# Zeroing PSUM tiles by matrix products and dealing a projection out in pairs, in a relational graph convolution on one Trainium2 core

## The chip, the cores and the metric

The kernel runs on one core of one Trainium2 chip (trn2). The metric is device time in microseconds (us) of one execution. Eight runs of the kernel before the change have a median of 3025.92 us (3016.6 to 3031.64). For this kernel a difference of about 0.2% (6 us) is what a measurement can tell from no change.

The engines are called PE (TensorE, the matrix products, with PEld for its weight loads), DVE (VectorE), ACT (ScalarE), POOL (GpSimd) and SP (SyncE, which here only issues DMAs). Matrix products land in PSUM.

## The reference

Two layers of a relational graph convolution with a residual, then a mixture of experts. N = 6250 nodes of D = 256 features, E = 100000 edges sorted by target, R = 8 relations; everything is f32.

```
seg  = dst * R + etype
sums = segment_sum(x[src], seg, N * R)            # one sum per (target node, relation)
cnt  = segment_sum(ones, seg, N * R)
mean = (sums / max(cnt, 1)).reshape(N, R, D)
y    = x @ Wroot + b + einsum('nrd,rde->ne', mean, W)
```

The first layer takes the layer norm of the input and ends in a relu, the second takes the first one's result. `h = x + y2` is then normalised again; a gate of 8 experts picks the best two of each row, and the weighted outputs of their two-layer networks (256 to 1024 to 256, with gelu) are added to `h`.

## The kernel before, in words

**Preparation** (until about 83 us). Nodes are normalised, each f32 row is split into three bf16 parts whose sum is the row, and these rows of 3 x 256 go to a table in DRAM (`xs`). The edges are turned into columns of indices.

**The two layers** (`layer(k)`, k = 0 from about 83 to 1156 us and k = 1 from there to about 2215 us). The edges lie in 782 tiles of 128 each, and the tiles in 194 groups of 1 to 6. The sums of a group span a window of at most 64 neighbouring nodes. For a group three things happen.

- `tiles_in` (L668 to L688) runs one group ahead of the sums. It takes one of two PSUM tiles `pg` and has ACT copy zeros into it (L672). For every edge tile POOL issues an indirect DMA (L680) that gathers the 128 source rows into one of 13 buffers `ge`, and DVE compares the tile's targets with a ramp (L686), which makes a matrix `oh` with a one where an edge meets its node and relation.
- `sums` (L691 to L700): for each edge tile, PE multiplies `ge` with `oh` in six products (two halves of the features, three bf16 parts; L696). All of them add to `pg`. In layer 0 a seventh product with a block of ones as weights (`ones16`, 128 x 128) makes the counts (L699). A product has 8 columns for each node of its tile's window, 140 on average.
- `add` (L702 to L715): DVE adds the window of `pg` to one of two rings of sums in SBUF (L710). The rings keep 3 blocks of 128 nodes each.

**A block of nodes** is projected when its sums are whole. The planner `_plan` reckons for every one of the 49 blocks the step (a step is one group) from which no later edge can reach it; this is `whole[b]`. Work on a block is due at fixed distances from that step: `root` at -1 (its own features), `counts` at 0, `invert` at 1, then at 2 `project`, `clear` and `finish`, at 3 `turn`, and at 4 `logits`. `project` (L770 to L795) is 18 f32 products of 128 x 256 for a full block, the root and 8 relations with two halves each, in five PSUM tiles `pr` of two relations (L783); two such tiles exist. DVE scales and adds them up in `h` (L791, L793). `clear` has ACT zero the block's part of the ring (L800). `finish` applies the relu and writes the block's rows for the next layer, or the output.

**The main loop** runs over the steps. In a step it first calls `tiles_in` of the next group, then `project` and `clear`, `turn`, `finish`, then `sums` of the step's group, `invert`, `logits`, `add`, and `root`, `counts`. That is the order in which the program states the work. The framework that builds the kernel gives every engine a stream of its own and orders it by when it reckons instructions to be ready; an engine's stream is then fixed, and an instruction that waits holds up all behind it in its stream. `bounds` in `_plan` says which blocks a group may touch; the kernel checks the edges against it before it takes this path, and dependencies that the bounds rule out are not waited for.

**The experts** follow from about 2215 us to the end, with 1024-wide f32 products (L1214, L1225).

Of the kernel before, what the change touches and what calls it, by code (L numbers as in the profile page):

```python
# [39 lines left out]
BF16 = mybir.dt.bfloat16  # L40
# [8 lines left out]
P = 128  # L49
# [45 lines left out]
Z = 4.8  # L95
WIN = 64
RB = 3
READ = 2
TAKE = 3
EARLY = 30  # L100

# [1 line left out]
def _plan(N, E, R):  # L103

    T = -(-E // P)

    def windows(ts, n):

        mid = n // 2
        lo, hi = [0] * n, [-(1 << 30)] * n
        for t in ts:
            for k in range(n + 1):
                i0, i1 = t * P, max(0, t + k - mid) * P
                mean = N * (i1 * i1 - i0 * i0) / (E * E)
                sd = 2 * N * i0 / (E * E) * math.sqrt(abs(i1 - i0)) + 0.004 * abs(mean)
                if k < n:
                    lo[k] = min(lo[k] if t != ts[0] else 1 << 30, math.floor(mean - Z * sd) - (k < mid))
                if k:  # L120
                    hi[k - 1] = max(hi[k - 1], math.ceil(mean + Z * sd) + (1 if k <= mid else 2))
        shift = -min(lo)
        w = [(a + shift, b + shift) for a, b in zip(lo, hi)]
        return shift, w, max(b for _, b in w)


    NB = -(-N // P)
    mid = max(0, round((N / 4 - P / 2) / P))
    split = round(T * math.sqrt((mid + 0.5) * P / N))
    regions = []  # L130
    t = 0
    while t < T:
        left = (split if t < split else T) - t
        for n in range(min(6, left), 0, -1):
            ng = max(1, min(36, left) // n)
            shift, w, width = windows((t + n // 2, t + n * (ng - 1) + n // 2), n)
            if width <= WIN:
                break
        regions.append((t, n, ng, shift, w, width))
        t += n * ng  # L140
    groups = []
    for r, (t0, n, ng, *_) in enumerate(regions):
        for g in range(ng):
            groups.append((t0 + g * n, n, r))
    NG = len(groups)
    up = [g for g in range(NG) if groups[g][0] < split]
    down = list(range(NG - 1, len(up) - 1, -1))
    size = [sum(groups[g][1] for g in s) for s in (up, down)]
    seq, at, n = [], [0, 0], [0, 0]
    while len(seq) < NG:  # L150

        s = int(n[1] * (size[0] - EARLY) < n[0] * size[1])
        if at[s] == len((up, down)[s]):
            s = 1 - s
        g = (up, down)[s][at[s]]
        seq.append(g)
        at[s] += 1
        n[s] += groups[g][1]
    step = {g: q for q, g in enumerate(seq)}

    whole = []
    for b in range(NB):
        if b == mid:
            whole.append(NG - 1)
            continue
        p = math.sqrt((b + 1 if b < mid else b) * P / N)
        dev = Z * math.sqrt(E * p * (1 - p)) + 1
        t = int(min(E - 1, E * p + dev) // P) if b < mid else int((E * p - dev) // P)
        whole.append(step[next(g for g, (t0, n, _) in enumerate(groups) if t0 + n > t)])


    bounds = []
    for g in range(NG):
        read, taken = ([b for b in range(NB) if whole[b] + n < step[g]] for n in (READ - 1, TAKE))
        if g < len(up):
            bounds.append((sum(b < mid for b in read) or -NB, sum(b < mid for b in taken) + RB))
        else:
            n = sum(b > mid for b in read)
            bounds.append((NB - sum(b > mid for b in taken) - RB, NB - n if n else 2 * NB))
    return T, regions, groups, seq, len(up), mid, whole, bounds  # L180
# [3 lines left out]
def kernel(  # L184
# [20 lines left out]
    nc = tc.nc  # L205
# [430 lines left out]
    with tc.If(go == 1) as cmp:  # L636
        with ExitStack() as arm:
# [4 lines left out]
            hTs = ap.tile([P, NB, KD, P], F32, name="hTs", bufs=1)  # L642
            zeros = ap.tile([P, WIN], F32, name="zeros", bufs=1)
            nc.vector.memset(zeros, 0.0)
            rings = [ap.tile([P, KD + 1, R, RING + WIN], F32, name=f"ring{i}", bufs=1) for i in range(2)]

            step = {g: q for q, g in enumerate(seq)}
# [8 lines left out]
            def layer(k):  # L656
# [11 lines left out]
                def tiles_in(g):  # L668
                    t0, n, r = groups[g]
                    pg = psum.tile([P, nd, R, WIN], F32, name="pg", tag="pg", bufs=2)  # L670
                    wd = regions[r][5]
                    state["zeroed"] = nc.scalar.copy(pg[:, :nd, :, :wd],  # L672
                                                     zeros[:, None, None, :wd].to_broadcast([P, nd, R, wd]))
                    got = []
                    ohs = ap.tile([P, OHW], BF16, name="oh", bufs=3)
                    o0 = 0
# [13 lines left out]

                def sums(g):  # L691
                    pg, got = state[g]
                    for ge, oh, m, a, b in got:
                        for c in range(KD):
                            for s in range(3):
                                nc.tensor.matmul(pg[:, c, :, a:b], ge[:m, s, c, :], oh, start=False, stop=False,  # L696
                                                 skip_group_check=True)
                        if nd > KD:
                            nc.tensor.matmul(pg[:, KD, :, a:b], ones16[:m], oh, start=False, stop=False,  # L699
                                             skip_group_check=True)  # L700

                def add(g):  # L702
                    pg, _ = state.pop(g)
# [59 lines left out]
                def invert(b):  # L763
                    if k == 0:
# [2 lines left out]
                        nc.vector.tensor_scalar(invs[:, b], pc[:, :R], 1.0, None, op0=OP.max)  # L767
                        nc.vector.reciprocal(invs[:, b], invs[:, b])

                def project(b):  # L770

                    n = rows(b)
# [3 lines left out]
                    h = ap.tile([P, D], F32, name="h", bufs=2)  # L776
                    lhs = [(R, [xT[:, c, :n] for c in range(KD)])]
                    lhs += [(r, [ring[:, c, r, s0 : s0 + n] for c in range(KD)]) for r in range(R)]
                    for i in range(0, R + 1, 2):
                        pr = psum.tile([P, 2, D], F32, name="pr", tag="mm", bufs=MM)  # L780
                        for j, (r, chunks) in enumerate(lhs[i : i + 2]):
                            for c in range(KD):
# [5 lines left out]
                        for j, (r, _) in enumerate(lhs[i : i + 2]):  # L788
# [3 lines left out]
                            else:  # L792
                                nc.vector.scalar_tensor_tensor(h[:n], pr[:n, j], invs[:n, b, r : r + 1], h[:n],  # L793
                                                               op0=OP.mult, op1=OP.add)
                    state["h", b] = h  # L795

                def clear(b):
# [47 lines left out]
                tiles_in(seq[0])  # L845
                due = {}
                for b, q in enumerate(whole):
                    for d, f in ((-1, root), (0, counts), (1, invert), (2, project), (2, clear), (2, finish), (3, turn), (4, logits)):
                        due.setdefault(q + d, []).append((f, b))

                todo = []
# [8 lines left out]
                def run(q, *fs):  # L860
                    for f, b in due.get(q, []):
                        if f in fs:
                            f(b)

                cleared[:] = [[(-1, ins) for _, ins in c] for c in cleared]
                for q in range(NG + 5):
                    if k == 1 and q == 2:

                        with tc.issue_after(state["zeroed"].ins):
# [4 lines left out]
                    if q == 0 and k == 0:  # L874
                        for c in range(KD + 1):
                            nc.vector.memset(rings[0][:, c], 0.0)
                            nc.scalar.copy(rings[1][:, c], zeros[:, None, 0:1].to_broadcast([P, R, RING + WIN]))
                    run(q, project, clear)
                    run(q, turn)
                    run(q, finish)  # L880
                    if q < NG:
                        sums(seq[q])
                    run(q, invert, logits)
                    if q < NG:
                        add(seq[q])
# [388 lines left out]
```

## Time and profile before

The profiled execution took 3019.99 us; its span, from the first to the last instruction, is 3018.2 us.

| | value |
|---|---|
| median of 8 runs | 3025.92 us |
| profiled execution, and its span | 3019.99 us, 3018.2 us |
| first gather of layer 0 and end of its last | 83.38 us, 1117.38 us |
| first gather of layer 1 and end of its last | 1155.50 us, 2154.01 us |
| gathers in each layer | 782 |
| ACT copies of zeros to `pg` (L672) | 388, 380.1 us in all, 981 ns each |
| ACT clears of the rings (L800) | 98, 227.8 us in all |
| counts products (L699) | 782, 241 ns each by their records |
| granted PE clock, mean over the span | 0.924 |

The granted clock is the share of full speed that PE was allowed at that moment. A record of a product runs from its start to its modelled end, so that records of a stream overlap: what a product costs a busy PE is read from one start to the next.

### The profile page before, as it was taken

The numbers are of one execution on the slowest core, as the hardware profiler recorded it, in microseconds if no ns is written. First come the engines' busy times: TensorE is split into PE (matmuls) and PEld (weight loads), VectorE is DVE, ScalarE is ACT, GpSimd is POOL, SyncE is SP. The second block draws the span as 40 slices with busy tenths as digits, with TensorE's granted clock in tenths as the row PEclk, the third lists the DMA queues.
The fourth block names the chain that finished last, engine by engine and source line by source line (L and its number), as shares of the span: only waits on it lengthen the run. The fifth ranks groups of instructions, "written<-read, shape, count | busy, mean of one in ns | idle before, by whom it ended". The sixth has DMA issues, their size and how long they took to land. (4 is left out here: it accounts for less than half of the span.)

```text
span 3018.2 us, 52037 instructions
## 1 busy us (share of the span) xinstructions
PE 2556.7 (85%) x18131; PEld 2160.1 (72%) x18131; DVE 1620.5 (54%) x4676; ACT 1019.1 (34%) x1378; POOL 1807.3 (60%) x2109
## 2 busy tenths in 40 slices
PE   5578887888889876888888888898839999999997
PEld 2466776776777765666766767777628888888886
DVE  7566676766666674666766776676711111111111
ACT  6434444443444332332323323232312222222221
POOL 1667777777776765777777777777413333333332
PEclk9689999999999997988989998999969999999999
DMA  7555665655565544666566666666364444444441
GB/s 250 156 147 166 169 173 165 171 163 169 166 175 159 163 138 142 177 176 173 167 173 176 173 177 174 174 183 173 109 201 113 118 109 107 109 120 107 107 122 19
DMA packets 215591, 461.05 MB, mean 153 GB/s; under 512 B 50716, under 2 KB 123222, under 8 KB 215190
## 3 DMA queue, kind: packets, MB, share of 16 engines
q0 software_dynamic: 120384, 334.45, 41.9%
q1 hardware_dynamic: 83724, 112.33, 11.2%
q10 hardware_dynamic: 11210, 10.81, 1.1%
q8 instruction: 149, 2.44, 0.3%
q14 instruction: 124, 1.02, 0.1%
HBM read 412.02 MB, written 46.31 MB: 152 GB/s over the span
## 5 line engine op out<-in xcount | busy, mean ns | idle before, releaser
L680 POOL DMA_INDIRECT ge<-xs,idx x1564 | 1518.2, 971 | 618.4 <-issue 224.3
L696 PE MATMUL pg<-oh,ge 128*128 128x200 bf16 (+24 forms) x9384 | 831.9, 241 | 308.7 <-DMA ge<-xs,idx 218.7
L696 PEld LDWEIGHTS <-ge 128*128 128x128 bf16 x9384 | 673.6, 105 | 431.4 <-DMA ge<-xs,idx 270.2
L783 PE MATMUL pr<-gw,ring 128*128 128x256 f32 (+1 forms) x3136 | 747.2, 393 | 1.3 <-DVE h L793 0.8
L783 PEld LDWEIGHTS pr<-gw,ring 128*128 128x128 f32 (+1 forms) x3136 | 612.1, 198 | 96.2 <-DVE h L793 4.7
L710 DVE TENSOR_TENSOR ring<-pg,ring 128x1176 f32 (+31 forms) x388 | 456.5, 1176 | 281.8 <-PE pg L696 141.5
L672 ACT COPY pg<-zeros 128x1176 f32<-128x1176 f32 (+31 forms) x388 | 380.1, 981 | 534.9 <-DVE ring L710 508.5
L793 DVE SCALAR_TENSOR_TENSOR h<-pr,invs,h 128x256 f32<-128x256 f32 (+1 forms) x784 | 376.5, 480 | 157.7 <-PE pr L783 140.0
L800 ACT COPY ring<-zeros 128x3072 f32<-128x3072 f32 (+1 forms) x98 | 227.8, 2324 | 675.3 <-PE pr L783 616.9
L1215 ACT ACTIVATE hT<-ph,bcol 128x256 f32<-128x256 f32 x424 | 200.8, 474 | 536.2 <-PE ph L1214 536.2
L1214 PE MATMUL ph<-xT,w 128*128 128x256 f32 x1696 | 378.2, 382 | 0.0
L1225 PE MATMUL po<-fw,hT 128*128 x1696 | 374.4, 379 | 0.0
L1225 PEld LDWEIGHTS po<-fw,hT 128*128 128x128 f32 x1696 | 322.2, 190 | 43.8
L1214 PEld LDWEIGHTS ph<-xT,w 128*128 128x128 f32 x1696 | 320.9, 192 | 42.2
L686 DVE TENSOR_SCALAR oh<-iota,rel 128x152 bf16<-128x152 f16 (+25 forms) x1564 | 335.9, 273 | 19.4 <-PE pg L699 14.1
L1186 POOL DMA_INDIRECT xg<-xnd,ti x106 | 105.4, 995 | 351.5 <-DMA ti<-tlist 264.8
L1230 POOL DMA_INDIRECT out_dram<-fo,ti x106 | 168.7, 1591 | 229.0 <-DVE wt L1199 108.3
L1228 DVE TENSOR_TENSOR fo<-po,b2b 128x256 f32<-128x256 f32 x106 | 45.0, 425 | 299.5 <-PE po L1225 299.5
L699 PE MATMUL pg<-oh,ones 128*128 128x128 bf16 (+24 forms) x782 | 188.5, 241 | 0.0
L1209 DVE COPY bcol<-b1c 128x8 f32 x53 | 9.0, 171 | 302.4 <-ACT hT L1215 301.9
L699 PEld LDWEIGHTS <-ones 128*128 128x128 bf16 x782 | 82.7, 106 | 2.7
L783 PE MATMUL pr<-gw,hTs 128*128 128x256 f32 (+1 forms) x196 | 70.8, 485 | 2.3 <-ACT hTs L831 2.1
(190 smaller groups left out, 1349.2 us busy)
## 6 DMA issues: line engine op xcount, KB each, us to landing
w<-in_L_ffn_W_dram SPq DMA_DIRECT2D x53, 1024.0 KB
ge<-xs,idx POOLq DMA_INDIRECT x1564
xt<-in_x_dram SPq DMA_DIRECT2D x96, 128.0 KB
xs<-xb SPq DMA_DIRECT2D x8, 1152.0 KB
xs<-hb SPq DMA_DIRECT2D x48, 192.0 KB
fw<-in_L_ffn_W_dram ACTq DMA_DIRECT2D x8, 1024.0 KB
xt<-in_x_dram SPq DMA_DIRECT2D x8, 768.0 KB
out_dram<-h SPq DMA_DIRECT2D x48, 128.0 KB
```

Source lines behind the costliest of these rows:

```text
L672: state["zeroed"] = nc.scalar.copy(pg[:, :nd, :, :wd], zeros[:, None, None, :wd].to_broadcast([P, nd, R, wd]))
L680: nc.gpsimd.indirect_dma_start(out=ge[:m].rearrange("p s k d -> p (s k d)"), out_offset=None, in_=xs[k][:, :], in_offset=bass.IndirectOffs ...
L686: nc.vector.tensor_scalar(oh, iota16[:m].rearrange("p (r d) -> p r d", r=R)[:, :, a:b], rel[:m, t : t + 1], None, op0=OP.is_equal)
L696: nc.tensor.matmul(pg[:, c, :, a:b], ge[:m, s, c, :], oh, start=False, stop=False, skip_group_check=True)
L699: nc.tensor.matmul(pg[:, KD, :, a:b], ones16[:m], oh, start=False, stop=False, skip_group_check=True)
L710: a = nc.vector.tensor_tensor(slot, pg[:, :nd, :, :wd], slot, OP.add).ins
L783: mm = nc.tensor.matmul(pr[:n, j], chunks[c], w[:, c, r, :], start=(c == 0), stop=(c == KD - 1))
L793: nc.vector.scalar_tensor_tensor(h[:n], pr[:n, j], invs[:n, b, r : r + 1], h[:n], op0=OP.mult, op1=OP.add)
L800: ins = nc.scalar.copy(at, zeros[:, None, None, 0:1].to_broadcast([P, nd, R, P]))
L1214: nc.tensor.matmul(ph[:, :TK], w1[:, k, h * P : (h + 1) * P], xT[:, k, :], start=(k == 0), stop=(k == KD - 1))
L1215: nc.scalar.activation(hT[:, h, :], ph[:, :TK], AF.Gelu, bias=bcol[:, h : h + 1], scale=1.0)
L1225: nc.tensor.matmul(po[:, :D], hT[:, k, f * P : (f + 1) * P], rhs, start=(k == 0), stop=(k == KH - 1))
```

## The change

Four edits belong together.

1. `tiles_in` has ACT zero `pg` only in the first three steps of a layer. From step 3 on, `sums` begins with one product for each slice of `pg` (three in layer 0, two in layer 1): `ones16` as weights and a tile of bf16 zeros as columns, with `start=True`, so that the slice is overwritten with zeros. Its width is 8 times the group's window, up to 512 columns.
2. The counts product takes one column of `ones16` as weights in place of all 128, and writes one row of `pg`.
3. `project` no longer issues its products; it puts five pairs of relations in a list. `sums` takes one pair from the list after each edge tile, and what is left is done when the group's tiles are through.
4. `project` is stated after `turn`, `clear` and `finish`; `clear` and `finish` move to distance 3, `turn` to 4 and `logits` to 5, and the loop has one step more. The planner counts a block as read one step earlier (`READ` goes) and leaves a quarter of a tile as margin in `whole`.

```diff
-READ = 2
-        dev = Z * math.sqrt(E * p * (1 - p)) + 1
+        dev = Z * math.sqrt(E * p * (1 - p)) + P / 4
-        read, taken = ([b for b in range(NB) if whole[b] + n < step[g]] for n in (READ - 1, TAKE))
+        read, taken = ([b for b in range(NB) if whole[b] + n < step[g]] for n in (0, TAKE))
+            zeros16 = ap.tile([P, R * WIN], BF16, name="zeros16", bufs=1)
+            nc.vector.memset(zeros16, 0.0)
...
-                    state["zeroed"] = nc.scalar.copy(pg[:, :nd, :, :wd],
-                                                     zeros[:, None, None, :wd].to_broadcast([P, nd, R, wd]))
+                    if step[g] < 3:
+                        state["zeroed"] = nc.scalar.copy(pg[:, :nd, :, :wd],
+                                                         zeros[:, None, None, :wd].to_broadcast([P, nd, R, wd]))
...
                 def sums(g):
                     pg, got = state[g]
+                    wd = regions[groups[g][2]][5]
+                    for c in range(nd if step[g] >= 3 else 0):
+                        nc.tensor.matmul(pg[:, c, :, :wd], ones16, zeros16[:, : R * wd].rearrange("p (r d) -> p r d", r=R),
+                                         start=True, stop=False, skip_group_check=True)
...
-                            nc.tensor.matmul(pg[:, KD, :, a:b], ones16[:m], oh, start=False, stop=False,
+                            nc.tensor.matmul(pg[0:1, KD, :, a:b], ones16[:m, 0:1], oh, start=False, stop=False,
                                              skip_group_check=True)
+                        go_on()
...
+                pairs = []
+                def go_on():
+                    if pairs:
+                        f, i = pairs.pop(0)
+                        f(i)
...
-                    for i in range(0, R + 1, 2):
+                    def pair(i):
                         pr = psum.tile([P, 2, D], F32, name="pr", tag="mm", bufs=MM)
...
+                    pairs.extend((pair, i) for i in range(0, R + 1, 2))
...
-                    for d, f in ((-1, root), (0, counts), (1, invert), (2, project), (2, clear), (2, finish), (3, turn), (4, logits)):
+                    for d, f in ((-1, root), (0, counts), (1, invert), (2, project), (3, clear), (3, finish), (4, turn), (5, logits)):
...
-                for q in range(NG + 5):
+                for q in range(NG + 6):
...
-                    run(q, project, clear)
-                    run(q, turn)
+                    run(q, turn, clear)
                     run(q, finish)
+                    run(q, project)
                     if q < NG:
                         sums(seq[q])
+                    while pairs:
+                        go_on()
```

With the new margin, `whole` moves for 2 of the 49 blocks, by one step each; the groups and their order stay as they are.

## The prediction

> **What bounds the kernel now.** I read the page first, its busy table, then the group of the gathers, then the busy time of each engine by windows that cut the two layers and the experts apart.
>
> ```profile
> PE 2556.7 (85%) x18131; PEld 2160.1 (72%) x18131; DVE 1620.5 (54%) x4676; ACT 1019.1 (34%) x1378; POOL 1807.3 (60%) x2109
> ...
> L680 POOL DMA_INDIRECT ge<-xs,idx x1564 | 1518.2, 971 | 618.4 <-issue 224.3
> ```
>
> PE looks like the bound and POOL like a bystander, but these are averages over three stages. In the timeline a gather takes 0.95 us and the next starts 0.30 us behind its end, whatever else happens: one per 1.25 us. 782 of them are 977.5 us, and a layer's gathers span 1034.0 us (83.38 to 1117.38) and 998.5 us (1155.50 to 2154.01). So **both layers run at the pace of POOL**. What they lose above it is small: in layer 0, 36 gathers longer than 1 us (24.2 us more than 0.95 each) and 31.2 us in which POOL waited beyond its 0.30 us for PE to give back a gather buffer; in layer 1, 12.4 us and 7.3 us. The largest of these waits is
>
> ```profile
> 948.18 0.94 POOL L680 DMA_INDIRECT ge<-xs,idx  x1 [6.37 <-PE pg L696]
> ```
>
> Only these 38.5 us can be won by a better order on PE, and only as long as PE keeps up. Does it? The windows of layer 0 (columns: length, busy of PE, PEld, DVE, ACT, POOL, then granted clock, DMA share, GB/s):
>
> ```profile
> 83.00:200.00 117.00, 79.11 (x652) 64.64 (x652) 71.23 (x149) 48.77 (x51) 81.19 (x83) 0.76 0.52 148
> ...
> 800.00:1000.00 200.00, 172.54 (x1498) 148.62 (x1495) 137.65 (x330) 85.27 (x96) 147.31 (x154) 0.94 0.60 169
> 1000.00:1117.00 117.00, 100.82 (x792) 86.45 (x793) 80.01 (x181) 44.71 (x46) 87.67 (x85) 0.91 0.56 155
> ...
> 2215.00:3018.00 803.00, 761.36 (x3604) 668.35 (x3604) 138.00 (x422) 202.06 (x425) 274.12 (x212) 0.97 0.44 114
> ```
>
> PE is busy 858 of 1034 us in layer 0 (the six windows from 83 to 1117 added up) and 836 of 998 in layer 1. It has 176 and 162 us to spare. The clock is low where PE idles (0.76 in the first window) and 0.97 where it hardly does (the experts), so more work raises it.
>
> **Part 1: zeros by products.** Out go 191 ACT copies in each layer (388 of 981 ns, less three in each layer that stay). ACT is 34% busy, so its time is worth nothing; what counts is who waits for it. PE does, 64.5 us in 60 waits in layer 0 and 14.6 us in 17 in layer 1:
>
> ```profile
> PE pg L696 <- ACT pg L672: 64.5, 60, 4.5
> ```
>
> Some of this wait is ACT standing in its queue before a clear of the ring that waits for a projection. It goes, but it is PE time that the gathers mostly hide, so the gain is a share of the 38.5 us. In come 191 x 3 = 573 products in layer 0 and 382 in layer 1. Their width is that of the additions (L710): by the planner's windows 392 columns on average. Price of a column, from six products of 160 in a stream:
>
> ```profile
> 949.37 0.58 PE L696 MATMUL pg<-oh,ge 128*128 128x160 bf16 x6
> ...
> 949.79 0.23 PE L699 MATMUL pg<-oh,ones 128*128 128x160 bf16 x1
> ```
>
> Six starts take 0.42 us: 0.07 us for 160 columns, 0.172 us for 392. That is **98 us more on PE in layer 0 and 66 in layer 1**. Upper end: the record of a bf16 product of 512 columns (L521, 402 ns with its modelled end), 230 and 154 us. Lower end: the ACT waits that go, taken off whole, 34 and 51 us. I take 98 and 66, because a busy PE pays starts and not records. What is new is the wait: a zeroing product waits for the addition of the group two before, and everything on PE is queued behind it, sums and pairs alike, and behind them the gather buffers. ACT waited for the same addition before and then took 1 us more, so for PE the wait gets shorter; it costs nothing while PE runs ahead of the gathers and up to some 0.5 us a group where it doesn't.
>
> **Part 2: the counts with one column of weights.** It looks like a saving: 782 products in layer 0 with less to load. The trace has the same form in the expert choice (L383, one column of `ones`), between products with 128 columns of weights:
>
> ```profile
> 2041.15 0.19 PE L380 MATMUL rpp<-roh,upper 128*128 128x64 bf16 x1
> ...
> 2041.18 0.18 PE L381 MATMUL rpp<-roh,ones 128*128 128x32 bf16 x1
> 2041.29 0.09 PEld L383 LDWEIGHTS <-ones 128*1 128x1 bf16 x2
> 2041.29 0.20 PE L383 MATMUL rpp<-roh,ones 128*1 128x32 bf16 x2
> ...
> 2041.43 0.25 PE L696 MATMUL pg<-oh,ge 128*128 128x168 bf16 x1
> ```
>
> L381 starts 0.03 us behind L380, whose 64 columns it has to let pass. L383 has only 32 columns to let pass and starts 0.11 us behind L381: its weight load isn't pulled ahead but begins when the array has run out. The next wide product starts 0.12 us behind the second L383 (2041.31; the two share a row). So going in costs 0.08 us more and coming out 0.09. L411 (8 columns of weights, also among L696) shows the same:
>
> ```profile
> 2116.01 0.34 PE L696 MATMUL pg<-oh,ge 128*128 128x184 bf16 x2
> ...
> 2116.27 0.08 PEld L411 LDWEIGHTS <-rnum 128*8 128x8 bf16 x1 [0.15 <-issue]
> 2116.28 0.22 PE L411 MATMUL rpl<-rcol,rnum 128*8 128x128 bf16 x1
> ...
> 2116.43 0.25 PE L696 MATMUL pg<-oh,ge 128*128 128x176 bf16 x1
> ```
>
> The second L696 starts at 2116.09 and needs 0.08 us; L411 comes at 2116.28, 0.11 late, and what follows it 0.10 late. A count in its new form therefore costs PE 0.17 to 0.21 us more than one with 128 columns, whose load (L699) lies in the shadow of the product before. I take 0.18: **141 us more on PE in layer 0**, none in layer 1, which has no counts. Ends: the weight load alone is 24 ns shorter (81 for 105), 19 us less; 0.21 us is 164 more.
>
> The Trainium skill, page "TensorE: Matmul & The Clock Gate", section "LDWEIGHTS (loading the stationary operand)", lets a weight load's time go with its columns (columns / 1.2 ns): one column would be an estimated 1 ns, and by that the change would save some 0.1 us a tile. The record of 81 ns speaks against it. The same page, section "Weight-path perf modes", says that the fast weight load needs 128 weights, which speaks against this edit; it gives no price for leaving it.
>
> **Part 3: pairs between tiles, and the later steps.** The same 18 products for a block and the same DVE work, in another order. A block's products take 36 records of 0.22 us, 7.9 us of PE in which gathers fill six of 13 buffers; with tiles in between, buffers come back earlier. In the stream of the changed kernel as built that is so for groups of five and six tiles; small groups do two pairs or three after their last tile. In the kernel before, the builder had mixed projections and sums in part already. The later `finish` and `turn` spare PE its waits for the relu (L830 on L808, 15.7 us in layer 0). All of this can win from the same 38.5 us. At the seam of the layers (38.1 us from the last gather to the next first one) and behind layer 1 the steps hang on the last block's chain; I count nothing there, within 3 us. The memset of `zeros16` is one small DVE instruction before the layers, under 0.5 us.
>
> **The sum.** Layer 0: PE has 858 + 98 + 141 = 1097 us of work at a clock of 0.92. With PE idle no more the clock should come near the experts' 0.97, so the old 858 shrink by 858 x (1 - 0.92/0.97) = 44, to 1053 us in all. POOL needs 977.5 + 24.2 = 1002. So **PE becomes the bound of layer 0**. Waits that aren't for gathers stay with it: the counts' transfer before a transpose (11.3 us), the first gathers (some 5), additions that zeroing waits for (say 14): 30. That makes 1083 us from the first gather to the last sum; before, it was 1038 (83.4 to 1121.5). Layer 0: +45. Layer 1: 836 + 66 = 902 us of PE against POOL's 990: still POOL's, with 7.3 us of buffer waits that may go or double: 0. Experts: 0. The profiled execution's 3020.0 would become 3065; the median of the runs lies 5.9 above that execution, which gives 3071. I say **3070**.
>
> **Rivals.**
> - **A, the forecast (0.62):** PE-bound layer 0, +20 to +80: 3045 to 3105.
> - **B, faster (0.15):** the narrow count costs next to nothing among the sums, because loads still overlap there. PE then has 858 + 98 - 44, about 912 us, and POOL keeps the layer; of the 38.5 us of buffer waits, half or more go: -20, 3006 (3000 to 3018). It decides from a round trip of about 0.06 us: 47 us more, under which PE's sum and waits stay below 1002. For it: L383 and L411 are few and sit at switches of work. Against it: both show the gap on both sides, and L411 sits among the very sums.
> - **C, near nothing (0.10):** half the price, 0.09 us a tile: PE at about 985 plus 30 of waits against POOL's 1002, gains and losses about even: 3020 to 3045.
> - **D, much slower (0.13):** in layer 0 PE also stands before zeroing products, because DVE, in order and two thirds busy (137.65 of 200), has comparisons and block sums ahead of the addition. 0.5 us on each of 191 groups is 95 us on top: 3105 to 3165. Layer 1 would add to it if its densest stretch goes past POOL's pace.
> - That pairs aren't dealt out as said is part of A: the builder orders them, and the order wins at most the 38.5 us.
>
> Range: A, C and the nearer part of D, 3018 to 3120; B (0.15) and the far end of D (0.04) are left out. About 0.2% (6 us) is what a measurement can tell from no change. Faster: B, 0.15. Same: the lower part of C, 0.06. Slower: 0.79.
>
> **What would show it.** In the new profile: POOL's waits for PE in layer 0 several times 31 us, the gathers' span there near 1080, PE's idle time in that layer gone and its clock above 0.92; count products that start 0.1 us late and are followed 0.1 us late; layer 1's gathers still within 10 us of 998. Wrong: a layer 0 at 1010 to 1030 us with 0.06 us steps around the counts (B), or PE waiting over 60 us for additions (D).

## The result, and the profile after

The changed kernel takes **3047.31 us** (median of 14 runs, 3039.05 to 3052.17), beside 3026.14 us (40 runs) for the kernel before. The ratio is 1.0069, with an interval of 1.0059 to 1.0079: slower by some 21 us. The forecast was 3070, so the sign and the stage were right; the forecast loss of 44 us was about twice the measured one. The profiled execution took 3046.83 us, its span is 3045.1 us (before: 3019.99 and 3018.2).

By stages, both profiled executions, from the first and last gathers on POOL and the last sum on PE:

| stage | before | after | difference | forecast |
|---|---|---|---|---|
| up to the first gather of layer 0 | 83.4 | 82.5 | -0.9 | 0 |
| layer 0, first gather to last sum | 1038.3 | 1072.9 | +34.6 | +45 |
| last sum to first gather of layer 1 | 33.8 | 29.8 | -4.0 | 0 |
| gathers of layer 1 | 998.5 | 989.8 | -8.7 | 0 |
| from there to the end | 864.2 | 870.1 | +5.9 | 0 |
| span | 3018.2 | 3045.1 | +26.9 | +45 |

The page of the changed kernel: the busy table, the chain that ended last by engine and by line, and the gathers, the counts and the zeroing products among the groups.

```profile
PE 2759.3 (91%) x19068; PEld 2190.5 (72%) x19086; DVE 1619.7 (53%) x4677; ACT 659.5 (22%) x996; POOL 1810.2 (59%) x2110
...
PE 78%; DMA 12%; DVE 3%; issue 2%; ACT 1%; POOL 1%; SPq 0%; DVEq 0%; ACTq 0%; POOLq 0%
PE pr L798 26%; PE pg L702 17%; PE ph L1232 12%; PE po L1243 12%; DMA ge<-xs,idx 9%; PE pg L697 4%; PE pg L705 4%; DVE ring L717 1%; PE pt L313 1%; PE pt L1216 1%; DMA xt<-in_x_dram 1%; DMA fw<-in_L_ffn_W_dram 1%; DMA cn<-ring 1%; PE pl L322 1%; POOL ge L682 0%
...
L682 POOL DMA_INDIRECT ge<-xs,idx x1564 | 1521.0, 972 | 636.5 <-issue 227.5
...
L697 PE MATMUL pg<-zeros,ones 128*128 128x392 bf16 (+17 forms) x937 | 236.8, 345 | 13.3 <-DVE ring L717 12.6
...
L705 PE MATMUL pg<-oh,ones 128*1 128x128 bf16 (+24 forms) x782 | 177.2, 227 | 0.0
```

PE's busy time rises by 203 us and the span by 27. The chain that ended last now runs 78% on PE, with the narrow counts (L705) and the zeroing products (L697) among its lines. The average hides where the time goes: the gathers keep their number and length. It is the windows of the changed kernel that show the turn (columns as in the prediction; the last row is the whole of layer 0, from the first gather to the last sum):

```profile
83.00:200.00 117.00, 96.83 (x734) 67.19 (x735) 73.29 (x155) 26.44 (x26) 82.84 (x85) 0.85 0.54 152
...
600.00:800.00 200.00, 196.18 (x1550) 144.67 (x1548) 132.56 (x315) 43.32 (x56) 145.77 (x150) 0.98 0.57 163
800.00:1000.00 200.00, 198.60 (x1495) 146.28 (x1494) 131.67 (x317) 42.04 (x54) 146.22 (x151) 1.00 0.58 164
1000.00:1144.00 144.00, 144.00 (x1073) 105.77 (x1071) 97.56 (x226) 34.50 (x41) 103.60 (x102) 1.00 0.54 155
...
2240.00:3045.00 805.00, 761.58 (x3604) 668.53 (x3604) 138.16 (x422) 201.99 (x425) 274.34 (x212) 0.97 0.45 115
...
82.50:1155.40 1072.90, 1034.95 (x7969) 759.25 (x7978) 707.42 (x1673) 235.25 (x291) 769.06 (x782) 0.98 0.56 159
```

Between 800 and 1000 us PE is busy 198.6 of 200 us where it was 172.5, and the granted clock is 1.00 where it was 0.94. Over layer 0 PE is busy 1035 of 1072.9 us. POOL, the bound before, now waits for PE: beyond its own 0.30 us it waits 55.4 us for buffers in layer 0 (31.6 before by the same count, which the prediction put at 31.2). The experts' window has not moved in busy time.

What PE still waits for in layer 0 (waits by engine and line, window 83 to 1144; us in all, times, longest):

```profile
PE pg L702 <- DMA ge<-xs,idx: 27.1, 10, 16.4
PE pg L697 <- DVE ring L717: 10.8, 9, 1.7
PE pc L773 <- DMA cn<-ring: 5.8, 6, 1.7
```

16.4 of the 27.1 us for gathers is the very first wait of the layer, and most of it lies ahead of the first gather at 82.5 us:

```profile
87.59 0.40 PE L702 MATMUL pg<-oh,ge 128*128 128x40 bf16 x6 [16.43 <-DMA ge<-xs,idx]
```

The 64.5 us that PE waited for ACT's zeroing are gone; 10.8 us for the additions have come in their place.

### The profile page after: what moved, and what is told of

It reads as the page before. It is cut to its first block, busy times and chain, and to the rows that moved or that the text cites. A ratio compares the mean times of both kernels' runs of the same rounds, so it can differ in the third digit from the quotient of the medians.

```text
span 3045.1 us, 53362 instructions
## 1 busy us (share of the span) xinstructions
PE 2759.3 (91%) x19068; PEld 2190.5 (72%) x19086; DVE 1619.7 (53%) x4677; ACT 659.5 (22%) x996; POOL 1810.2 (59%) x2110
## 3 DMA queue, kind: packets, MB, share of 16 engines
q1 hardware_dynamic: 83724, 112.33, 11.2%
## 4 chain that ended last, share of the span: by engine, by line
PE 78%; DMA 12%; DVE 3%; issue 2%; ACT 1%; POOL 1%; SPq 0%; DVEq 0%; ACTq 0%; POOLq 0%
PE pr L798 26%; PE pg L702 17%; PE ph L1232 12%; PE po L1243 12%; DMA ge<-xs,idx 9%; PE pg L697 4%; PE pg L705 4%; DVE ring L717 1%; PE pt L313 1%; PE pt L1216 1%; DMA xt<-in_x_dram 1%; DMA fw<-in_L_ffn_W_dram 1%; DMA cn<-ring 1%; PE pl L322 1%; POOL ge L682 0%
## 5 line engine op out<-in xcount | busy, mean ns | idle before, releaser
L702 PE MATMUL pg<-oh,ge 128*128 128x200 bf16 (+24 forms) x9384 | 864.6, 235 | 147.0 <-DMA ge<-xs,idx 140.3
L702 PEld LDWEIGHTS <-ge 128*128 128x128 bf16 x9384 | 643.2, 101 | 318.4 <-DMA ge<-xs,idx 171.1
L798 PE MATMUL pr<-gw,ring 128*128 128x256 f32 (+1 forms) x3136 | 765.4, 389 | 2.4 <-DVE h L808 2.4
L798 PEld LDWEIGHTS pr<-gw,ring 128*128 128x128 f32 (+1 forms) x3136 | 586.0, 193 | 87.7 <-DVE h L808 3.8
L697 PE MATMUL pg<-zeros,ones 128*128 128x392 bf16 (+17 forms) x937 | 236.8, 345 | 13.3 <-DVE ring L717 12.6
L705 PE MATMUL pg<-oh,ones 128*1 128x128 bf16 (+24 forms) x782 | 177.2, 227 | 0.0
L705 PEld LDWEIGHTS <-ones 128*1 128x1 bf16 x782 | 61.9, 79 | 99.9 <-issue 52.7
L697 PEld LDWEIGHTS <-ones 128*128 128x128 bf16 x955 | 83.4, 103 | 51.6 <-issue 14.1
```

The lines of the kernel that those rows point to most:

```text
L697: nc.tensor.matmul(pg[:, c, :, :wd], ones16, zeros16[:, : R * wd].rearrange("p (r d) -> p r d", r=R), start=True, stop=False, skip_group_c ...
L705: nc.tensor.matmul(pg[0:1, KD, :, a:b], ones16[:m, 0:1], oh, start=False, stop=False, skip_group_check=True)
L798: mm = nc.tensor.matmul(pr[:n, j], chunks[c], w[:, c, r, :], start=(c == 0), stop=(c == KD - 1))
```

## The experiments

**Two kinds of chip.** Some of the runs came on chips on which the kernel before itself takes 3.79 to 3.83 ms, with a granted clock of 0.845, so each number below is a ratio to the kernel before on the same chip, and the argument rests on the chip where that kernel takes 3025.59 us, as it does beside the result (3026.14). I call that one the chip of the result, though which chip the result itself came from is not known, and the others (three by their numbers) the 3.8 ms chips. The changed kernel itself was not run on a 3.8 ms chip.

### 1. The changed kernel with wide counts

Theory: the narrow counts make PE the bound; undone, POOL bounds layer 0 again and the kernel is faster than both. Rival: the zeroing products or the pairs do it, and little changes.

```
-  nc.tensor.matmul(pg[0:1, KD, :, a:b], ones16[:m, 0:1], oh, ...)
+  nc.tensor.matmul(pg[:, KD, :, a:b], ones16[:m], oh, ...)
```

> The changed kernel with one edit undone: the counts are again products with 128 columns of weights. Theory (PE bounds layer 0 of the changed kernel, and the 0.18 us that each of 782 narrow counts costs, 141 us of PE, is what tips it): PE's work in layer 0 falls from 1035 us to about 895, under POOL's 1002; the layer's gathers span about 1010 to 1020 us instead of 1062, and the time falls below the kernel before, to about 3005 (2995 to 3015). Rival 1 (the zeroing products with their 98 us and their wait for DVE's additions make the layer long): no change against the changed kernel, 3040 to 3050. Rival 2 (the new order of the block's steps costs the time): also 3040 to 3050.

> The changed kernel with counts of 128 columns of weights, again, since the first run fell on a chip where the kernel before takes 3829 us. On a chip like that of the prediction: theory (PE bounds layer 0 by the narrow counts): layer 0's gathers span 1010 to 1020 us, ratio to the kernel before 0.990 to 0.997. Rivals (zeroing products, or the order of the steps): ratio 1.004 to 1.010 as for the changed kernel. On a chip like the last one the theory says little, since gathers and not PE set the pace there; the ratio would be about 0.96 again.

On the chip of the result (e1b): 3008.47 us, ratio **0.9957** [0.994, 0.9973], faster than both kernels. Layer 0's gathers span 1023.1 us, 38.7 less than in the changed kernel; layer 1's 992.7. The expectation for layer 0 was 1010 to 1020, a little too low. This is the prediction's rival B with its condition made true: it gave PE 912 us of work in layer 0 and the kernel 3006. The window of layer 0 and PE's longest waits in it (83 to 1117 us) in that variant:

```profile
83.00:1117.00 1034.00, 916.73 (x7978) 767.22 (x7978) 709.12 (x1681) 234.05 (x293) 767.63 (x782) 0.95 0.58 165
```

```profile
PE pg L702 <- DMA ge<-xs,idx: 75.5, 73, 16.1
PE pc L773 <- DMA cn<-ring: 20.5, 18, 2.5
PE pg L697 <- DVE ring L717: 19.9, 23, 1.7
```

917 us busy, and PE waits for gathers 73 times, not 10: POOL bounds again, and the zeroing products alone do not fill PE. On a 3.8 ms chip (e1): 3678.4 beside 3829.4, 0.9609 [0.9583, 0.9635], a gain some nine times as large, to which experiment 4 comes back.

### 2. The narrow counts alone

```
-  nc.tensor.matmul(pg[:, KD, :, a:b], ones16[:m], oh, ...)        # in the kernel before
+  nc.tensor.matmul(pg[0:1, KD, :, a:b], ones16[:m, 0:1], oh, ...)
```

> The kernel before with the narrow counts alone. Theory: 141 us more of PE in layer 0, 805 at a raised clock and 141, 946 in all, and the waits for ACT's copies (64 us) on top: PE about at POOL's pace of 1002 us, layer 0 longer by 10 to 30 us; 3035 to 3055. If the price of a narrow count is nothing among the sums: 3026 within 6.

> The kernel before with narrow counts alone, on a chip like that of the prediction. Theory: PE's work in layer 0 rises by about 141 us to some 946 at a raised clock, the waits for ACT's copies stay; ratio 1.003 to 1.010, with layer 0 alone longer, by 10 to 30 us. If narrow counts are harmless: 1.000 within 0.002. On a chip like the last one: 1.00 to 1.005.

On the chip of the result (e3b): 3059.04 us, **1.0114** [1.0082, 1.0146], some 34 us more and more than the whole change costs. The gathers of layer 0 span 1078.4 us, 44 more than before where 10 to 30 were expected, with 76.9 us of buffer waits. Layer 1, which has no counts and is unchanged, has 1002.7 for 998.5: two profiles of the same work differ by 4 us there. (The profiled run, 3065.45 us, was the longest of its four.) PE's longest waits in layer 0 there (83 to 1144 us):

```profile
PE pg L696 <- DMA ge<-xs,idx: 46.7, 50, 16.0
PE pg L696 <- ACT pg L672: 43.2, 37, 5.0
```

With ACT zeroing, PE has waits beside its work that it can no longer hide: 43 us for ACT. The changed kernel has these no more and 100 us of zeroing products instead, and is not slower than this one. On a 3.8 ms chip (e3): 1.0018 [0.9996, 1.0041].

### 3. The zeroing products alone, and without them

```
+  if step[g] < 3:                                # e4, e4b: in the kernel before
       state["zeroed"] = nc.scalar.copy(pg[:, :nd, :, :wd], ...)
...
+  for c in range(nd if step[g] >= 3 else 0):
+      nc.tensor.matmul(pg[:, c, :, :wd], ones16, zeros16[:, : R * wd]..., start=True, stop=False, ...)
```

e2 is the changed kernel with ACT zeroing in every step and no zeroing products.

> The kernel before with the zeroing products alone, counts with 128 columns, order of the steps as before. Theory: PE's work in layer 0 is about 903 us, under POOL's 1002, and its waits for ACT's copies go: 3010 to 3026. Rival 1 (zeroing by products is what costs): 3040 to 3060.

> The kernel before with zeroing products alone, on a chip like that of the prediction. Theory: PE has about 903 us in layer 0 against POOL's 1002, waits for ACT's copies go: ratio 0.994 to 1.000. Rival 1 (zeroing by products costs the time): 1.004 to 1.012. On a chip like the last one: 1.00 to 1.005.

> The changed kernel with one edit undone: ACT zeroes the sums' tiles in all steps; narrow counts and pairs stay. Theory: PE's work in layer 0 falls by 98 us to about 937, under POOL's 1002, but PE waits for ACT's copies come back; layer 0 ends near that of the kernel before, 3015 to 3035. Layer 1 loses part of the 9 us that it won. Rival 1 (zeroing products are the cause): the whole loss of 21 us goes, 3005 to 3025, and more than in the run with wide counts. Rival 2 (order): 3040 to 3050.

On the chip of the result (e4b): 3021.48 us, 0.999 [0.9974, 1.0007], no difference that can be measured. Layer 0's gathers 1033.2 us (before 1034.0), layer 1's 1004.1 (998.5). On a 3.8 ms chip (e4) 1.0016 [0.9998, 1.0033]. e2 ran on a 3.8 ms chip only, 0.9694 [0.9667, 0.9722]; without the changed kernel beside it there, it says nothing on the products' worth.

Their price per column was right. Two rows of the changed kernel's timeline:

```profile
700.69 0.62 PE L697 MATMUL pg<-zeros,ones 128*128 128x344 bf16 x3
...
701.15 0.50 PE L702 MATMUL pg<-oh,ge 128*128 128x128 bf16 x6
```

Three products of 344 columns take 0.46 us start to start, 0.446 ns a column; the prediction used 0.172/392 = 0.439.

### 4. Pairs and later steps

e5 is the kernel before with edits 3 and 4 alone. e10 and e10c are e5 with the projection done whole, so that the later steps remain:

```
   run(q, project)
+  while pairs:
+      go_on()
   if q < NG:
       sums(seq[q])
-  while pairs:
-      go_on()
```

> The kernel before with the pairs and the later steps alone (ACT zeroes, counts of 128 columns). Theory: PE has no work more; part of the 38.5 us of buffer waits goes, the tail behind layer 1 gets some us longer: ratio 0.992 to 1.000. Rival 2 (the new order costs the time): 1.004 to 1.010. On a chip like the last one the pairs would be what gave the changed kernel with wide counts its 4%: 0.95 to 0.97; if instead the zeroing and the pairs give it only together, 0.98 to 1.00.

> The kernel before with the later steps alone: finish, clear at 3, turn at 4, logits at 5, the projection stated behind them but whole, ahead of the sums; ACT zeroes, counts of 128 columns. Theory (what wins is that PE no longer waits for the relu and the normalised rows, 15.7 us of waits for L830 in layer 0, and that a block's products don't hold up gather buffers behind those waits): most of the 13 us that pairs and steps won together, ratio 0.995 to 0.998. Rival (dealing the pairs out between tiles wins it, because buffers come back earlier): 0.998 to 1.002.

> The kernel before with the later steps alone, the projection whole ahead of the sums. On the chip of 3.8 ms it gave 0.9996 where pairs and steps with wide counts gave 0.961, so dealing out is what wins there. On a chip like that of the prediction: if the pairs win here too, 0.998 to 1.002; if the later steps do, 0.995 to 0.998.

e5, on the chip of the result: 3012.54 us, **0.9958** [0.9941, 0.9974], a gain of 13 us where the prediction counted none. POOL's longest waits for PE in layer 1 (window 1160 to 2185) show half of it. Before, with these two edits alone, and in the changed kernel:

```profile
POOL ge L680 <- PE pg L696: 113.7, 349, 6.1
```

```profile
POOL ge L681 <- PE pg L698: 103.7, 332, 2.0
```

```profile
POOL ge L682 <- PE pg L702: 100.5, 330, 0.3
```

The last number is the longest wait. 0.3 us is POOL's own step, so in the changed kernel hardly a gather of layer 1 waits for a buffer. Summed beyond 0.30 us: 7.8 us before, 2.9 with these edits alone, 0.4 in the changed kernel. The gathers span 998.5, 992.3 and 989.8 us. On the chip of the result the three kernels with edits 3 and 4 have 989.8 to 992.7 there (e1b the last), the three without 998.5 to 1004.1, so this gain is more than the 4 us by which unchanged work differs. In layer 0 e5 gains 6.0 us (1028.0 for 1034.0), by one profile each.

The steps alone ran on 3.8 ms chips only: 0.9996 [0.997, 1.0023] and 0.9998 [0.9978, 1.0018], nothing. The zeroing products alone give nothing there either (e4), yet all edits but the narrow counts give 0.961 (e1), and without the zeroing products, with narrow counts, it is still 0.969 (e2). That leaves the pairs for the most of it, by subtraction; pairs without the later steps were not run. That the 0.4% on the chip of the result is also the pairs' and not the steps' is likely, but no run there separates them.

### 5. How many columns make a count dear

The changed kernel with 127 and with 64 columns of weights in the counts:

```
-  nc.tensor.matmul(pg[0:1, KD, :, a:b], ones16[:m, 0:1], oh, ...)
+  nc.tensor.matmul(pg[0:127, KD, :, a:b], ones16[:m, 0:127], oh, ...)      # e8: 0:64
```

> The changed kernel with 127 columns of weights in the counts. If every weight load of fewer than 128 columns loses its place in the shadow of the product before: the step into and out of a count is as long as with one column (together 0.17 to 0.2 us more than with 128), layer 0's gathers span about 1062 us. If only weights that leave part of the array's columns unused in blocks are late: as with 128, about 1023 us. I take the first to be the likelier.

> The changed kernel with 64 columns of weights in the counts. By both readings of a late weight load (fewer than 128 columns; part of the array left out) the gap stays: layer 0's gathers about 1062 us. If the gap grew with the columns left out, 0.08 to 0.1 us in all: 1030 to 1045 us.

Each ran once, on a 3.8 ms chip: 3672.15 (127) and 3682.34 us (64), with layer 0's gathers at 1347.7 and 1368.6 us (1349.5 in e1). The rows tell more. Each fence has six products of 112 columns, the count behind them, and the next tile's six (start, length, engine). One column, the changed kernel:

```profile
701.73 0.47 PE L702 MATMUL pg<-oh,ge 128*128 128x112 bf16 x6
702.13 0.08 PEld L705 LDWEIGHTS <-ones 128*1 128x1 bf16 x1
702.13 0.21 PE L705 MATMUL pg<-oh,ones 128*1 128x112 bf16 x1
...
702.27 0.39 PE L702 MATMUL pg<-oh,ge 128*128 128x80 bf16 x6
```

128 columns, the variant with wide counts:

```profile
651.13 0.46 PE L702 MATMUL pg<-oh,ge 128*128 128x112 bf16 x6
651.38 0.10 PEld L705 LDWEIGHTS <-ones 128*128 128x128 bf16 x1
651.43 0.21 PE L705 MATMUL pg<-oh,ones 128*128 128x112 bf16 x1
...
651.48 0.46 PE L702 MATMUL pg<-oh,ge 128*128 128x96 bf16 x6
```

127 columns:

```profile
751.43 0.46 PE L702 MATMUL pg<-oh,ge 128*128 128x112 bf16 x6
751.68 0.14 PEld L705 LDWEIGHTS <-ones 128*127 128x127 bf16 x1
751.73 0.22 PE L705 MATMUL pg<-oh,ones 128*127 128x112 bf16 x1
...
751.79 0.46 PE L702 MATMUL pg<-oh,ge 128*128 128x96 bf16 x6
```

64 columns:

```profile
798.07 0.46 PE L702 MATMUL pg<-oh,ge 128*128 128x112 bf16 x6
798.45 0.11 PEld L705 LDWEIGHTS <-ones 128*64 128x64 bf16 x1
798.46 0.24 PE L705 MATMUL pg<-oh,ones 128*64 128x112 bf16 x1
...
798.62 0.47 PE L702 MATMUL pg<-oh,ge 128*128 128x96 bf16 x6
```

Read the starts. From the six to the count: 0.40, 0.30, 0.30 and 0.39 us; from the count to the next six: 0.14, 0.05, 0.06 and 0.16. Six times 112 columns at 0.45 ns are 0.30 us. With 128 and 127 columns the load begins 0.05 us ahead of its product and lies beside the sums; with 1 and 64 it begins with its product, some 0.1 us after the sums ahead of it have had their 0.30. So 127 columns behave as 128, against the expectation taken as the likelier. The rows stand for the rest: over all counts of layer 0 the load begins 0.067 us ahead of its product (median) with 128 columns and 0.068 with 127, and 0.002 us with 64 and with one. Beyond 0.446 ns a column, the median step into a count (703 with six sums of equal width ahead) is 0.003 us with 128 columns, 0.004 with 127, 0.100 with 64 and 0.098 with one; the step out (480, to another sum) 0.005, 0.013, 0.125 and 0.097. So one column costs 0.10 on the way in and 0.09 on the way out, 0.19 us; the prediction took 0.18. 782 such counts are 149 us of PE.

### 6. Narrow counts put together

If the switch between full and narrow weights is what costs, counts that follow one another share it. The changed kernel with the counts of a group in a loop of their own, behind the group's other products:

```
   for ge, oh, m, a, b in got:
       ...                                        # six products
       go_on()
+  for ge, oh, m, a, b in got if nd > KD else []:
+      nc.tensor.matmul(pg[0:1, KD, :, a:b], ones16[:m, 0:1], oh, ...)
```

> The changed kernel, counts with one column of weights, but all counts of a group in a row behind the group's other products. Theory (the price is the change between wide and narrow weights and back, 0.18 us each time): 191 round trips in place of 782, 34 us of PE in place of 141, PE at about 930 us against POOL's 1002: layer 0's gathers span 1020 to 1035 us, ratio 0.996 to 1.000. Rival (every narrow product has its price, whatever stands beside it): as the changed kernel, 1062 us and ratio 1.005 to 1.009.

> As e9, on a chip like that of the prediction: counts with one column of weights, but all of a group's in a row. Theory (the price is the step between wide and narrow weights, 0.10 us in and 0.10 us out by the rows of the changed kernel): 191 round trips, 37 us of PE in layer 0; its gathers span 1025 to 1040 us, ratio 0.996 to 1.001. Rival (each narrow product pays by itself): 1062 us, 1.005 to 1.009.

> Counts with one column of weights, all of a group's in a row. On a chip like that of the prediction: layer 0's gathers 1025 to 1040 us and ratio 0.996 to 1.001 if the price belongs to the step between widths, 1062 us and 1.005 to 1.009 if every narrow product pays.

On 3.8 ms chips only: 0.9714 [0.9695, 0.9733], 0.9703 [0.9654, 0.9752], 0.9732 [0.9698, 0.9766]. Wide counts (e1, another 3.8 ms chip) had 0.9609, and layer 0's gathers span 1373.7 us in e9 for 1349.5 there. Grouped narrow counts do not come back to the wide ones there. The rows of e9 settle the price itself. The last sums of a group, then its counts:

```profile
728.52 0.69 PE L702 MATMUL pg<-oh,ge 128*128 128x88 bf16 x11
729.13 0.40 PE L706 MATMUL pg<-oh,ones 128*1 128x96 bf16 x6
```

Six narrow counts in a row take 0.40 us, where a single one of 112 columns has a record of 0.21: the five steps between them take 0.18 us for their 400 columns, 0.46 ns a column. Over the 580 steps from count to count in e9 the median excess over 0.446 ns a column is 0.001 us, while the step from sums into a row of counts keeps its 0.100. So the price belongs to the change between wide and narrow weights, as the theory said, and not to every narrow product. How much time the grouping saves against scattered counts stays open, since the changed kernel was not run on these chips.

### 7. The end of layer 1

The stage behind layer 1's gathers is 5.9 us longer after the change. On the chips where the kernel before takes some 3026 us, all kernels with edits 3 and 4 have it longer (870.1, 870.3 in e1b, 867.0 in e5) than those without (864.2, 858.5 in e4b, 862.1 in e3b). In the changed kernel's timeline, its sums done, PE stands 3.06 us before the transpose of a layer norm's rows (L313), with the next block's projection (L798) queued behind it; in the kernel before, sums run through at the like place. After, then before:

```profile
2183.33 0.46 PE L702 MATMUL pg<-oh,ge 128*128 128x112 bf16 x6
...
2186.85 0.69 PE L313 MATMUL pt<-ident,r 128*128 128x128 f32 x2 [3.06 <-DVE r L307]
...
2187.33 1.06 PE L798 MATMUL pr<-gw,hTs 128*128 128x256 f32 x2
```

```profile
2156.78 3.67 PE L696 MATMUL pg<-oh,ge 128*128 128x112 bf16 x52
```

The variant (e1 with this on top) states the projection ahead of the later steps' work once the groups are through:

```
+  if q >= NG:
+      run(q, project)
+      while pairs:
+          go_on()
   run(q, turn, clear)
   run(q, finish)
-  run(q, project)
   if q < NG:
+      run(q, project)
       sums(seq[q])
```

> The changed kernel with counts of 128 columns, and past the last group (where there are no sums to put pairs between) the projection is stated first again, ahead of turn, clear and finish. Theory: the stretch from layer 1's last gather to the end of the span, 864.2 us in the kernel before, 870.1 in the changed one and 870.3 with wide counts, shrinks by 4 to 7 us, since PE no longer stands before a transpose that waits for the normalised rows of the block before; ratio to the kernel before 0.993 to 0.995 against 0.9957 for wide counts alone. Rival (the longer tail comes from PE's larger backlog at the last gather): unchanged, 0.9957 within 0.001.

> As e6, on a chip like that of the prediction: the changed kernel with counts of 128 columns and, past the last group, the projection stated first. Theory: the stretch behind layer 1's last gather, 870 us, shrinks by 4 to 7 us; ratio 0.993 to 0.995. Rival (PE's backlog): 870 within 2 us, ratio 0.9957 within 0.001. On the chip of 3.8 ms the ratio was 0.966.

> The changed kernel with counts of 128 columns and, past the last group, the projection stated first. On the chip of 3.8 ms the ratio was 0.966 and 0.967, no better than 0.961 with the order unchanged. On a chip like that of the prediction: 0.9957 within 0.0015 if the order past the last group doesn't matter, 0.993 to 0.994 if it costs the 6 us by which the stretch behind layer 1 grew.

On 3.8 ms chips only: 0.9661 [0.9637, 0.9685], 0.9669 [0.9629, 0.9708], 0.9641 [0.9618, 0.9664]. The stage takes 877.9, 876.1 and 875.4 us, against 876.0 in e1: no gain where 4 to 7 us were expected. So the order at the end is not shown to be the cause, and the cause of the 5.9 us stays open: they come with edits 3 and 4 in the six kernels above, and how was not found.

### What the 3.8 ms chips do differently

There a layer's gathers span 1310 to 1435 us, 1.7 to 1.8 us each, with 325 to 450 us a layer in which POOL waits beyond its 0.30 us. Three lines from the waits of e3, layer 0 (window 83 to 1510):

```profile
ACT pg L672 <- issue: 149.0, 48, 8.3
...
DVE ring L710 <- remote: 96.8, 19, 12.8
...
PE pg L696 <- issue: 62.0, 88, 4.2
```

Engines stand before work for which nothing that the profile shows makes them wait ("issue"), or wait for an event whose sender it does not name ("remote"). In layer 0 of the kernel before on the chip of the result the first two do not occur, and the third is 0.2 us, once. What causes the pauses was not found. Kernels with pairs take 2.7 to 3.9% less there whatever their counts (e1, e2, e6 to e9; e7 and e8 by one run each); the changed kernel, which was not run there, would then be faster on such a chip. That is argued, not shown.

## Why the prediction was right in sign and wrong in size

**What bounds the kernel: right.** Both layers ran at POOL's pace, and PE had 176 us to spare in layer 0.

**Part 2, the narrow count: right.** 0.18 us assumed, 0.19 measured in the rows. Taking it out of the changed kernel gives back 38.7 us of gathers; putting it alone into the kernel before costs 34 us. This one edit makes the change slower.

**Part 1, the zeroing products: right.** 0.446 ns a column for 0.439. The wait for additions was put at some 14 us and came to 10.8, so rival D, which needed over 60, is refuted.

**PE becomes the bound of layer 0: right.** With PE's work at 1053 us and 30 us of waits the prediction had 1083 us; measured are 1035 us busy and 38 us idle, 1072.9. That this is so near is partly luck: the two terms miss in opposite ways, as the next part shows.

**Where it failed: the step called "The sum".** Its terms were mis-sized in four places, all towards too slow a kernel but one.

- *Layer 0, the old work and the waits: +45 forecast, +34.6 measured.* The prediction let the clock rise to the experts' 0.97, which shrank the old 858 us of work to 814. Over the layer it was 0.98, and 0.98 to 1.00 from 200 us on. Less 100 us of zeroing products (573 of 392 columns at 0.446 ns) and 149 of narrow counts, 786 of the 1035 us are the old work. The clock explains a fall to 805 (858 x 0.92/0.98). The other 19 are not shown; what fits is that a record has a modelled end which counts as busy only ahead of a gap (0.16 us in the prediction's row of six: 0.58 for 0.42), and that PE waited for gathers and ACT 157 times before and some 10 times after: 147 x 0.16 = 24 us. So the work was 18 us too high and the waits 8 too low. The prediction listed waits "that aren't for gathers" beside the first gathers' 5 us. The first gathers did take 5 us of the layer (16.4 less the 11.4 that lie ahead of it), but nine later waits for gathers add 10.7 us, seven of them before 150 us, in the stretch where PE is busy only 97 of 117 us; the counts' transfer (5.8 us for 11.3) and the additions came to less than listed.
- *Layer 1, and Part 3's new order: 0 forecast, -8.7 measured.* The sum let layer 1's 7.3 us of buffer waits "go or double: 0". They went: 7.8 us to 0.4, the rest is shorter long gathers (12.4 us to 11.2). Edits 3 and 4 alone give 13 us by medians (experiment 4). The prediction had named the 38.5 us these edits could win from and then taken none of it.
- *The seam, -4.0, and the tail, +5.9,* of which Part 3 said "I count nothing there, within 3 us". After the change the last sum of layer 0 ends 11.1 us behind the last gather (4.3 before), but what follows it is shorter. The tail's cause is open (experiment 7).
- *From the profiled execution to the median.* 5.9 us were added because the execution before lay that far below its median. The execution after lies 0.5 us below its own. This alone is 5.4 of the miss.

Together, with 0.9 us at the first gather: 10.4 + 8.7 + 4.0 + 0.9 - 5.9 + 5.4 = 23.5, which is 3070.9 less 3047.3 but for rounding. The largest, layer 0's, is shown as a size; what the last 19 us of its old work are is not.

**What the prediction said would show it.** Counts 0.1 late on both sides, PE's idle time in layer 0 down from some 176 us to 38, the clock above 0.92, layer 1 within 10 us of 998: all seen. "POOL's waits several times 31 us" and gathers "near 1080" were not: 55.4 and 1061.8. That sentence did not follow from the prediction's own sum even: 1080 less 977.5 and 24.2 is 78 us of waits, two and a half times.

**The edits by themselves.** On the chip of the result narrow counts give +34, zeroing products -3 (not to be told from nothing), pairs and later steps -13: +18, for a change that measures +21. Within their intervals the edits add up.

## What to carry to other kernels

Where one engine sets the pace and another has slack, sum the other's new work at the clock it will have when it is full: here 250 us of new PE work cost layer 0 35 us, since 176 us of slack and a rising clock took most of the rest. Weights with 64 columns or one were dearer here than full ones: look at the start-to-start times around an instance in the trace before narrowing a product among full ones, and where narrow products are needed, put them in a row (shown for PE's steps, not for the kernel's time). And a wait that a change can only shorten should be priced at some share of what it is, not at nothing.

## What the runs showed of the hardware

- **The length of a weight load does not tell its price.** The load of 127 columns has the longest record (0.14 us, 0.10 for 128, 0.11 for 64, 0.08 for one) and costs some 0.01 us more than that of 128; those of 64 and 1 cost 0.22 and 0.19 (medians of experiment 5). The price goes with whether the load begins ahead of its own product, beside the one before. Widths between 64 and 127 were not run.
- **The price is one of changing between wide and narrow weights.** Narrow counts in a row follow one another at some 0.45 ns a column, and only the step into the row costs 0.10 us more (experiment 6); the step out of a count costs the like (experiment 5).
- The Trainium skill, page "TensorE: Matmul & The Clock Gate", section "Weight-path perf modes — Fast Weight Load (FWL) and DoubleRow", makes the fast load depend on the number of weights being 128. The longer record at 127 agrees with that; the starts do not make it the price, since 127 columns cost PE almost nothing and 64 columns do.
- **The granted clock is 0.98 to 1.00** in the windows of layer 0 in which PE is busy 98% and more (0.94 at 86% in the kernel before). The experts' 0.97 (at 95%) was no ceiling.
- **Chips differ.** The same kernel takes 3025.59 us on one chip and 3829.4 on another, and the changed kernel with wide counts gains 0.4% on the first and 4% on the second.
